# One more accumulating transfer in the first round of each attention unit, and one sum product fewer on PE

## The chip, the core and the metric

The kernel runs on one core of a Trainium2 chip. The metric is the device time of one execution in microseconds (us): the median of three runs. A profile is one further execution of the same program. The engines are named as the profile names them: PE multiplies matrices (PEld is its weight load), DVE and ACT work on vectors, POOL works on vectors and issues the software DMA queue, SP issues most of the other transfers.

## What is computed

The reference is one layer on x of shape (2, 2048, 512): a layer norm, attention with a residual, a second layer norm and a product with weights in fp8, again with a residual. The change lies in the attention alone:

```python
q = (x @ wq + bq).reshape(b, s, 16, 32)      # 16 heads of 32
k, v = ...                                   # 2 groups of 32, each shared by 8 heads
scores = einsum('bqhd,bkhd->bhqk', rope(q) * 32**-0.5, rope(k)) * 32**-0.5
attn = softmax(scores, axis=-1)
out = einsum('bhqk,bkhd->bqhd', attn, v).reshape(b, s, d)
```

The softmax is a division: the exponentials times v, over the sum of the exponentials along the keys. The change is in how that sum is formed.

## The kernel before, in words

**Units and rounds.** The queries are cut into 8 blocks of 512. A unit is 4 heads times half a block (256 queries), so there are 64 units, and the loop at L975 takes them in order. A unit goes over the 2048 keys in 16 chunks of 128, four to a round, so four rounds (r = 0 to 3, L991). I call them the first to the fourth.

**One chunk.** `probabilities` (L946) lets PE form the scores T, keys on partitions (L960), less the maximum of each query, and ACT takes the exponential into a tile `p` of 128 x 4 x 256 in float32 (L969). `columns` (L905, matmuls at L910) multiplies v by the four `p` tiles of a round and accumulates in the first half of the PSUM tile `avs`. Meanwhile the scores of the next unit are formed a second time the other way round, queries on partitions, only for their maxima (L517 on PE, L524 on DVE). These pieces (`next(scores)`) stand between the others in a fixed order.

**The sums of the exponentials.** They need the sum over all 16 chunks and over the 128 partitions.
- POOL adds chunks 0 and 1 of a round into a tile called `pair`, and chunks 2 and 3 into a tile that is kept in the list `far_sums` (`add_pair` L934, the sum at L943).
- A transfer from SBUF to SBUF, issued by POOL, adds `pair` to that kept tile (L1014, `accum_op=ALU.add`, 512 KB). So each round leaves one kept tile: `far_sums[0]` to `far_sums[3]`, named pa_2, pa_6, pa_10 and pa_14 by their chunk.
- In the third round a second such transfer adds `far_sums[0]` to `far_sums[1]` (L1016).
- Three tiles are left per unit: 1, 2 and 3. They are called `far_before` in the next unit, where PE adds them over the partitions with a matrix of ones (`sum_up` L920, the matmuls at L924) into the second half of the next unit's `avs`: tiles 1 and 2 after the columns of the first round (L1027), tile 3 after those of the second (L1029). One tile is 4 products, 8 instructions in the profile.
- `finish_heads` (L881) then copies that half (L885), takes reciprocals (L889) and multiplies (L890).

**The order.** Within the loop everything is in the order written (`manual_schedule`): each engine takes its own instructions in that order, and the semaphores hold it until what it needs is there. Small jobs of the other stages (projections, rope, the output product, statistics) are put in by `fill` (L762), at most so many pieces per place. The software queue's transfers are issued by POOL in its order, after its sums and before the job pieces of that round. SP's queue brings the next head group's queries (L355) and, at the start of a block, the next blocks of x (L141) and of its normalized form (L371).

**Buffers.** The kept tiles have four buffers, `pair` two, `p` four. A buffer is free when the last reader of its former tile is done; for a transfer that is its landing.

Of the kernel before, what the change touches and what calls it, by code (L numbers as in the profile page):

```python
# [13 lines left out]
ALU = mybir.AluOpType  # L14
# [13 lines left out]
def preln_attn_fp8_ffn_kernel(  # L28
# [37 lines left out]
    nc = tc.nc  # L66
# [42 lines left out]
    def s_bank():  # L109

        if s_next[0] == lent[0]:
            s_next[0] = (s_next[0] + 1) % S_BANKS
        tag = f"s{s_next[0]}"
        s_next[0] = (s_next[0] + 1) % S_BANKS
        return tag
# [383 lines left out]
    def split_maxima():  # L499

        if split:
            mview, mx = split.pop()
            nc.gpsimd.tensor_tensor(  # L503
                mview[:, :, :, 1], mx, mview[:, :, :, 0].bitcast(F32), ALU.subtract
            )
# [32 lines left out]
    def gather_maxima(u):  # L538

        split_maxima()  # L540
        tp = ps_s.tile([P, TB], F32, tag=s_bank(), name=f"mtp_{u}")
        for i in range(HT):
            nc.tensor.transpose(
                tp[:, i * P : (i + 1) * P], mrow[:, i * P : (i + 1) * P].bitcast(F32), ident
            )
        mT = wide.tile([P, HB], F32R, tag="mT", name=f"mT_{u}")
        nc.scalar.copy(mT, tp[:, :HB])
        maxima[u] = mT
# [213 lines left out]
    def fill(kind, pieces=1):  # L762

        for _ in range(pieces):
            ready = [job for job in queue if job.due <= step[0] and not job.waits()]
            if lent[0] is not None:
                ready = [job for job in ready if job is owner[0]]
            able = [
                (jobs, job)
                for jobs, some in ((finishing, finishing[:1]), (queue, ready), (beside, beside))  # L770
                for job in some
                if job.kind in (kind, OTHER) and job.due <= step[0]
            ]
            if able:
                do(*able[0])
# [41 lines left out]
    def stack_next(u):  # L817
        k, half = units[u]
        n, quad = quads[k]

        if half == 0:
            if k + 1 < len(quads) and k + 1 not in qst:
                while quads[k + 1] not in q_raw:
                    advance()
                stack_queries(k + 1)
            b = batch(k)
            if b + 1 < B and n == (b + 1) * NB - 1:
                if quad == 2:
                    while (b + 2) * NB - 1 not in keys_done:
                        advance()  # L830
                    fetch_keys("kS", b + 1, 0)
                    fetch_keys("dkS", b + 1, 0)
            if b > 0 and n == b * NB and quad == 0:
                fetch_keys("kS", b, 1)
                fetch_keys("dkS", b, 1)
# [84 lines left out]
    def sum_up(dst, parts, start, stop):  # L920

        for i, part in enumerate(parts):
            for j in range(4):
                nc.tensor.matmul(  # L924
                    dst[j * HD : (j + 1) * HD, :],
                    ones,
                    part[:, j, :],
                    start=start and i == 0,
                    stop=stop and i == len(parts) - 1,
                    tile_position=(0, j * HD),  # L930
                    skip_group_check=True,
                )

    def add_pair(u, kc, a, b):  # L934
        far = kc % ROUND == 2
        pa = papool.tile(
            [P, 4, HB],
            F32,
            tag="pa" if far else "pair",
            name=f"pa_{u}_{kc}",  # L940
            bufs=4 if far else 2,
        )
        nc.gpsimd.tensor_tensor(pa, a, b, ALU.add)  # L943
        return pa

    def probabilities(u, T, kc):  # L946

        k, half = units[u]
        if kc < 2:
            for j in range(4):  # L950
                nc.tensor.matmul(  # L951
                    T[:, j, :],
                    sel[:, j, :],
                    maxima[u],
                    start=(j % 2 == 0),
                    stop=True,
                    skip_group_check=True,
                )
        for j in range(0, 4, 2):
            nc.tensor.matmul(  # L960
                T[:, j : j + 2, :],
                stacked["dkS"][:, group(k), kc * P : (kc + 1) * P],
                qst[k][:, j : j + 2, half * HB : (half + 1) * HB],
                start=False,
                stop=True,
                skip_group_check=True,
            )
        p = ppool.tile([P, 4, HB], F32, tag="p", name=f"p_{u}_{kc}")
        nc.scalar.activation(p, T, AF.Exp, scale=SCALE)  # L969
        return p  # L970

    with tc.manual_schedule():
        for _ in range(LEAD):
            next(scores)
        for u, (k, half) in enumerate(units):  # L975
            n, quad = quads[k]
            if half == 0 and quad == 0:
                attn_of[n] = wide.tile(
                    [P, QUADS, TB], F32, tag="attn", name=f"attn_{n}", bufs=2
                )  # L980
            stack_next(u)
            banks = [
                ps_t.tile([P, 4, HB], F32, tag="EO"[parity], name=f"T_{u}_{parity}")
                for parity in range(2)
            ]

            far_sums = []
            whole = u == len(units) - 1
            ending_soon = u >= len(units) - 2
            pieces = 2 if ending_soon else 1  # L990
            for r in range(ROUNDS):  # L991
                chunks = list(range(r * ROUND, (r + 1) * ROUND))
                step[0] += 1
                while r == 1 and landing:
                    landing.pop()()
                if r == 2:
                    ask(u)
                last = r == ROUNDS - 1
                next(scores, None)
                probs = [probabilities(u, banks[kc % 2], kc) for kc in chunks[:2]]  # L1000
                pair = add_pair(u, chunks[0], *probs)
                next(scores, None)
                if r > 0:
                    fill(ON_PE, pieces)
                probs.append(probabilities(u, banks[0], chunks[2]))
                next(scores, None)
                probs.append(probabilities(u, banks[1], chunks[3]))
                if last and u + 1 < len(units):
                    gather_maxima(u + 1)
                if ending_soon:  # L1010
                    fill(ON_DVE)
                if not (last and whole):
                    far_sums.append(add_pair(u, chunks[2], *probs[2:]))
                    nc.gpsimd.dma_start(out=far_sums[r], in_=pair, accum_op=ALU.add)  # L1014
                if r == 2:
                    nc.gpsimd.dma_start(out=far_sums[1], in_=far_sums[0], accum_op=ALU.add)  # L1016
                fill(ON_PE, pieces)
                next(scores, None)
                split_maxima()
                fill(ON_DVE, 3 if finishing else 2)  # L1020
                if r == 0:
                    avs = ps_av.tile([P, 2, HB], F32, tag="av", name=f"avs_{u}")
                columns(u, chunks, probs, avs[:, 0, :])


                if u > 0 and r == 0:
                    sum_up(avs[:, 1, :], far_before[1:3], False, False)  # L1027
                elif u > 0 and r == 1:
                    sum_up(avs[:, 1, :], far_before[3:], False, True)  # L1029
                    finishing.append(Job(finish_heads(u - 1, both, avs[:, 1, :])))  # L1030
            both = w2.tile([P, 2, HB], F32, tag="both", name=f"both_{u}", bufs=1)
            nc.scalar.copy(both[:, 0, :], avs[:, 0, :])  # L1032
            far_before = far_sums
        sums = ps_s.tile([P, TB], F32, tag=s_bank(), name="sums_last")[:, :HB]
        sum_up(sums, [pair, *probs[2:], *far_sums[1:]], True, True)
        finishing.append(Job(finish_heads(u, both, sums)))
        fetch_y_over_keys(2, "kS", 1)
        attending[0] = False
        for jobs in (finishing, queue, beside):
            while jobs:  # L1040
                jobs[0].step()
                if jobs[0].kind is None:
                    jobs.pop(0)
# [122 lines left out]
```

## Time and profile before

| what | value |
|---|---|
| three runs | 2355.38, 2356.63, 2365.41 us; median 2356.63 |
| the profiled execution | 2365.06 us, span from first to last instruction 2363.3 us |
| mean granted PE clock | 0.969 |
| the loop over the units | about from 118 to 2260 us of the span |
| PE busy in that stretch | 2029 of 2142 us |
| DVE, ACT, POOL busy there | 1562, 1150, 1723 us |
| DMA share of the 16 engines there | 0.61 |
| L1014 and L1016 transfers | 255 and 64, 512 KB each |
| L943, one sum on POOL | 2459 ns |
| ACT waiting for a POOL sum | 19.0 us in all |

How to read it: a row of the groups gives line, engine, operation, written tile <- read tiles, shape and count; then busy time in us and mean ns of one; then the engine's idle time just before them and what ended it. A row of the timeline gives start and length in us, engine, line, operation and count, and in brackets the idle time before it with its releaser. PE's matmuls overlap, so the step from one row's start to the next row's start tells more than the length. An issue of a transfer is a short instruction on POOL or SP; "to landing" is the time from issue until the data are there.

### The profile page before, as it was taken

What the parts mean: (1) busy time and instruction counts of PE and PEld (TensorE: products, weight loads), DVE (VectorE), ACT (ScalarE), POOL (GpSimd) and SP (SyncE); (2) the same over time, 40 slices, a digit from 0 to 9 for tenths busy, and PEclk for the clock granted to TensorE, in tenths of its full rate; (3) what the DMA queues carried; (4) which work ended last, traced back from release to release, by engine and by line L of the source; (5) the groups of instructions that cost most, each with busy time, mean ns of one, the idle gap of its engine ahead of it and who ended that gap; (6) DMA issues with size and microseconds to landing.
All of it is one profiled execution on the core that took longest, in us unless ns stands there. A gap on an engine that the chain in (4) does not pass through costs nothing. (4 is left out here: it accounts for less than half of the span.)

```text
span 2363.3 us, 39392 instructions
## 1 busy us (share of the span) xinstructions
PE 2145.0 (91%) x15506; PEld 1246.7 (53%) x15506; DVE 1697.7 (72%) x2679; ACT 1231.3 (52%) x1545; POOL 1765.8 (75%) x1199
## 2 busy tenths in 40 slices
PE   5499999999999999999999999999999799899855
PEld 2255555555555555555555555555555455555422
DVE  3467777776687676867767778676876977768378
ACT  2146555655556555645445556454555445555536
POOL 3268889888777987878778878787887777878700
PEclk9689999999999999999999999999999999999977
DMA  6546656666465666657486556564565646847502
GB/s 195 163 102 136 134 117 163 137 138 136 89 167 123 152 134 143 158 116 163 96 204 139 111 118 154 121 120 96 132 146 116 143 91 140 166 85 199 108 32 111
DMA packets 116410, 312.76 MB, mean 132 GB/s; under 512 B 16896, under 2 KB 17536, under 8 KB 112384
## 3 DMA queue, kind: packets, MB, share of 16 engines
q0 software_dynamic: 50160, 175.66, 39.6%
q1 hardware_dynamic: 63648, 133.21, 19.1%
q8 instruction: 121, 1.98, 0.4%
q10 hardware_dynamic: 2416, 1.38, 0.2%
q14 instruction: 65, 0.53, 0.1%
HBM read 91.56 MB, written 42.99 MB: 57 GB/s over the span
## 5 line engine op out<-in xcount | busy, mean ns | idle before, releaser
L524 DVE TENSOR_REDUCE part<-s 128x1 f32<-128x512 f32 x2048 | 1304.8, 683 | 559.6 <-PE s L517 546.0
L943 POOL TENSOR_TENSOR pa<-p,p 128x1024 f32<-128x1024 f32 x511 | 1233.5, 2459 | 300.6 <-ACT p L969 272.7
L969 ACT ACTIVATE p<-T 128x1024 f32<-128x1024 f32 x1024 | 1001.3, 1024 | 590.6 <-PE T L960 564.1
L517 PE MATMUL s<-kS,qst 128*128 128x512 f32 x2048 | 832.4, 465 | 97.0 <-DVE part L524 31.0
L960 PE MATMUL T<-qst,dkS 128*128 128x512 f32 x2048 | 669.7, 423 | 14.4 <-ACT p L969 14.3
L517 PEld LDWEIGHTS s<-kS,qst 128*128 128x128 f32 x2048 | 369.0, 190 | 488.4 <-DVE part L524 256.9
L910 PE MATMUL avs<-p,vX 128*32 128x256 f32 x8192 | 497.7, 383 | 0.8 <-ACT p L969 0.8
L960 PEld LDWEIGHTS T<-qst,dkS 128*128 128x128 f32 x2048 | 365.5, 189 | 161.8 <-ACT p L969 59.4
L910 PEld LDWEIGHTS avs<-p,vX 128*32 128x32 f32 x8192 | 239.7, 110 | 210.4 <-issue 64.7
L1014 POOL DMA_DIRECT2D pa<-pa x255 | 224.3, 880 | 80.4 <-POOL pa L943 75.3
L889 DVE RECIPROCAL both<-both 128x128 f32<-128x128 f32 x128 | 112.4, 919 | 33.8 <-ACT both L885 33.8
L301 PE MATMUL po<-wo_sb,attn 128*128 128x512 f32 x256 | 130.5, 601 | 0.9 <-DVE x_res L574 0.9
L301 PE MATMUL pq<-xnT_q,wq_sb 128*128 128x512 f32 x224 | 113.9, 592 | 0.0
L924 PE MATMUL avs<-pa,ones 128*32 128x256 f32 x1512 | 105.6, 382 | 5.6 <-DMA pa<-pa 5.6
L1032 ACT COPY both<-avs 128x256 f32<-128x256 f32 x64 | 23.8, 373 | 138.3 <-PE avs L910 137.1
L885 ACT COPY both<-avs 128x256 f32<-128x256 f32 x63 | 23.5, 373 | 131.9 <-PE avs L924 131.9
L890 POOL TENSOR_TENSOR attn<-both 128x256 f32<-128x256 f32 x64 | 85.0, 1328 | 6.8 <-DVE both L889 6.8
L951 PEld LDWEIGHTS T<-mT,sel 128*128 128x128 f32 x512 | 80.0, 192 | 12.2 <-issue 0.4
L951 PE MATMUL T<-mT,sel 128*128 128x256 f32 x512 | 82.9, 285 | 0.0
L1016 POOL DMA_DIRECT2D pa<-pa x64 | 74.0, 1156 | 6.5 <-DMA pa<-pa 6.2
L924 PEld LDWEIGHTS avs<-pa,ones 128*32 128x32 f32 x1512 | 49.1, 111 | 39.0 <-DMA pa<-pa 6.5
L503 POOL TENSOR_TENSOR mrow<-mx,mrow 128x8 fp32r<-128x8 f32 x64 | 52.8, 824 | 11.6 <-ACT mrow L532 11.6
(126 smaller groups left out, 1118.7 us busy)
## 6 DMA issues: line engine op xcount, KB each, us to landing
pa<-pa POOLq DMA_DIRECT2D x319, 512.0 KB, 4.7
qst<-q_far SPq DMA_DIRECT2D x128, 256.0 KB, 4.7
x_kv<-in_L_attn_x_dram SPq DMA_DIRECT2D x8, 1024.0 KB, 8.8
q_far<-hi_q SPq DMA_DIRECT2D x32, 256.0 KB, 4.3
q_far<-lo_q SPq DMA_DIRECT2D x32, 256.0 KB, 3.6
x_res<-in_L_attn_x_dram SPq DMA_DIRECT2D x8, 1024.0 KB, 12.3
x_res<-in_L_attn_bo_dram POOLq DMA_DIRECT2D x8, 1024.0 KB, 12.0
out_dram<-v SPq DMA_DIRECT2D x16, 512.0 KB, 2.8
```

The source lines that it names most:

```text
L301: nc.tensor.matmul(dst, lhs(c), rhs(c), start=(c == 0), stop=(c == chunks - 1))
L517: nc.tensor.matmul(s, qst[k][:, j, at : at + P], stacked["kS"][:, group(k), kb * TB : (kb + 1) * TB], start=True, stop=True,)
L524: nc.vector.tensor_reduce(part[:, i, j, kb : kb + 1], s, AX.X, ALU.max)
L889: nc.vector.reciprocal(piece, piece)
L890: nc.gpsimd.tensor_tensor(attn_of[n][:, quad, half * HB : (half + 1) * HB], both[:, 0, :], both[:, 1, :], ALU.mult)
L910: nc.tensor.matmul(av[j * HD : (j + 1) * HD, :], vX[batch(k)][:, kc, group(k), :], p[:, j, :], start=(kc == 0), stop=(kc == NTS - 1), tile ...
L924: nc.tensor.matmul(dst[j * HD : (j + 1) * HD, :], ones, part[:, j, :], start=start and i == 0, stop=stop and i == len(parts) - 1, tile_pos ...
L943: nc.gpsimd.tensor_tensor(pa, a, b, ALU.add)
L951: nc.tensor.matmul(T[:, j, :], sel[:, j, :], maxima[u], start=(j % 2 == 0), stop=True, skip_group_check=True,)
L960: nc.tensor.matmul(T[:, j : j + 2, :], stacked["dkS"][:, group(k), kc * P : (kc + 1) * P], qst[k][:, j : j + 2, half * HB : (half + 1) * H ...
L969: nc.scalar.activation(p, T, AF.Exp, scale=SCALE)
L1014: nc.gpsimd.dma_start(out=far_sums[r], in_=pair, accum_op=ALU.add)
```

## The change

In the first round of every unit but the first, POOL issues one more accumulating transfer: the preceding unit's tile 2 (pa_10) is added to its tile 3 (pa_14), just after that round's own L1014. PE's sum product of tile 2 in the first round goes away; the product of tile 3 in the second round now reads the joined tile.

```diff
                     nc.gpsimd.dma_start(out=far_sums[r], in_=pair, accum_op=ALU.add)
+                if r == 0 and u > 0:
+
+                    nc.gpsimd.dma_start(out=far_before[3], in_=far_before[2], accum_op=ALU.add)
                 if r == 2:
                     nc.gpsimd.dma_start(out=far_sums[1], in_=far_sums[0], accum_op=ALU.add)
...
                 if u > 0 and r == 0:
-                    sum_up(avs[:, 1, :], far_before[1:3], False, False)
+                    sum_up(avs[:, 1, :], far_before[1:2], False, False)
                 elif u > 0 and r == 1:
                     sum_up(avs[:, 1, :], far_before[3:], False, True)
```

Over the 63 units that have a predecessor this is 63 more transfers of 512 KB on POOL's queue, and 504 matmul instructions fewer on PE, with as many weight loads. All other instructions stay in their order on every engine. The joined tile's product waits for the landing of the new transfer. In the changed kernel the new transfer is L1017 and the third round's second transfer moves from L1016 to L1019.

## The prediction

> **What bounds the kernel now.** I read the page first: busy shares and costliest groups, then the POOL and DMA rows that the edit touches.
>
> ```profile
> PE 2145.0 (91%) x15506; PEld 1246.7 (53%) x15506; DVE 1697.7 (72%) x2679; ACT 1231.3 (52%) x1545; POOL 1765.8 (75%) x1199
> ...
> L924 PE MATMUL avs<-pa,ones 128*32 128x256 f32 x1512 | 105.6, 382 | 5.6 <-DMA pa<-pa 5.6
> ...
> L1016 POOL DMA_DIRECT2D pa<-pa x64 | 74.0, 1156 | 6.5 <-DMA pa<-pa 6.2
> ```
>
> PE is busy 91% of the span and 9 in 10 in nearly every slice, so PE sets the pace. L924 is the line that the edit shortens: today it waits for a transfer only 5.6 us in all. Next the timeline of PE over the first two rounds of unit 27.
>
> ```profile
> 1014.36 1.93 PE L910 MATMUL avs<-p,vX 128*32 128x256 f32 x32
> 1016.11 1.05 PE L924 MATMUL avs<-pa,ones 128*32 128x256 f32 x16
> 1017.09 0.72 PE L517 MATMUL s<-kS,qst 128*128 128x512 f32 x2
> ...
> 1022.82 1.93 PE L910 MATMUL avs<-p,vX 128*32 128x256 f32 x32
> 1024.57 0.61 PE L924 MATMUL avs<-pa,ones 128*32 128x256 f32 x8
> 1025.12 0.72 PE L517 MATMUL s<-kS,qst 128*128 128x512 f32 x2
> ```
>
> Two sum products are 16 instructions and take 0.98 us until the next line's start (1017.09 - 1016.11); one takes 0.55. One product is 0.43 us.
>
> **What is removed.** 63 units x 0.43 = 27 us of PE. It shortens the run only where the others idle at that point. In each unit I took the idle time of DVE between the start of the L910 columns and its next reduce, and counted at most that: 25 us. (In three units DVE has work throughout and nothing is gained; in three it idles 0.2 or less, in the others 0.39 and more.) ACT idles over 3 us there in every unit but the last. Gain 25, bounds 15 and 27.
>
> **What is added on POOL.** 63 issues. Where one follows another issue (L1014, then L1016) POOL goes on 0.58 us later: 36 us of POOL, which is 75% busy and waits 272.7 us for ACT before its sums. Queued behind the issue are the rope or statistics of a job and the next round's first sum; ACT waits for such sums 19.0 us in all. Cost 1, bounds 0 and 5. The new issue itself waits for the last landing on the fourth sum: that had come before the place of the new issue in 62 of 63 units, in one 0.7 us after it; nothing added. The third sum's buffer is now freed by a landing instead of PE, two rounds ahead of its next use: nothing.
>
> **What is added on the path.** PE's product in the second round (the 1024.57 line) now needs the new transfer landed, and it stands in PE's order: scores, T and columns wait behind it, and DVE, ACT and POOL behind those. The time it has: from the first round's L1014 issue to that product. The time it needs: today's third round issues two transfers in the same way. The groups of L1014 and of L1016, each by its source line:
>
> ```profile
> DMA to landing us min/median/max: 4.5/4.6/14.6
> ```
>
> ```profile
> DMA to landing us min/median/max: 6.2/6.7/16.8
> ```
>
> In the 64 third rounds the second lands 2.56 us (median) after the first, and 7.13 us after the first's issue when the queues are quiet (4.55 + about 2.56). Here a rule speaks for the change. The Trainium skill, page "DMA: Bandwidth & Descriptors", section "Anatomy of one DMA — SWDGE (gpsimd) path", gives about 2.0 us fixed plus bytes over 436 GB/s: by estimate 1.2 us for each 512 KB, both landed after 4.4 us. With that the sum of waits below is 7 us and the change wins. The rows show 2.56 per transfer, more than twice, so I take the rows.
>
> Now each unit's time from L1014's issue to the product, less 0.43 because PE arrives earlier. Two patterns, from the timelines of POOL (units 25 and 27) and PE (unit 25):
>
> ```profile
> 954.34 0.86 POOL L1014 DMA_DIRECT2D pa<-pa  x1 [0.30 <-POOL pa L943]
> ...
> 1016.99 0.88 POOL L1014 DMA_DIRECT2D pa<-pa  x1 [0.30 <-POOL pa L943]
> ```
>
> ```profile
> 959.77 0.61 PE L924 MATMUL avs<-pa,ones 128*32 128x256 f32 x8
> ```
>
> Unit 27 has 7.58 us, just enough (7.58 - 0.43 = 7.15). Unit 25 has 5.43: it waits 7.13 + 0.43 - 5.43 = 2.13. Half the units have other traffic. In unit 16, SP's queue loads the next queries and two blocks, and that unit's L1014 lands after 11.6 us instead of 4.5:
>
> ```profile
> 651.77 1.86 SPq L355 DMA_DIRECT2D qst<-q_far  x4
> 653.67 0.43 SPq L141 DMA_DIRECT2D x_kv<-in_L_attn_x_dram  x1
> 654.15 0.50 SPq L371 DMA_DIRECT2D xnT_q<-xnT_far  x1
> ```
>
> The wait there is 11.56 + 2.55 + 0.43 - 7.59 = 6.95. Done for all 63 units, with landing = the larger of 7.13 and L1014's own landing + 2.55:
> - 32 quiet units (landing under 5 us): 12 with less than 7 us wait 29, the other 20 nothing to speak of: 30 us.
> - 31 units beside loads: 15 with less than 7 us wait 79, the others 45: 124 us.
>
> Together 154 us in about 42 waits. Bounds: 67 if every unit were quiet; 189 if the second transfer takes 3.2 us beside loads, as the slowest fifth of the third rounds has it.
>
> **The clock.** Such waits have a second price. Unit 58 already has one today (the timeline of PE, then the busy time by stretches: length; PE, PEld, DVE, ACT, POOL; granted clock, DMA share, GB/s):
>
> ```profile
> 2061.70 1.94 PE L924 MATMUL avs<-pa,ones 128*32 128x256 f32 x16 [5.19 <-DMA pa<-pa]
> ```
>
> ```profile
> 2061.00:2063.00 2.00, 1.30 (x15) 0.59 (x16) 0.00 (x0) 0.00 (x0) 1.21 (x1) 0.50 0.98 234
> 2063.00:2065.00 2.00, 2.00 (x11) 1.16 (x4) 0.60 (x1) 0.00 (x0) 1.70 (x2) 0.50 0.99 216
> 2065.00:2067.00 2.00, 2.00 (x9) 1.48 (x7) 1.34 (x4) 1.29 (x2) 0.33 (x1) 0.89 1.09 222
> ```
>
> After 5.19 us of waiting the clock is half until about 2065.5. From that product to the next columns is 8.33 us (2061.70 to 2070.03) against 6.71 in unit 27 (1016.11 to 1022.82): 1.6 us dearer. The Trainium skill, "TensorE: Matmul & The Clock Gate", section "Part 1: The HAM clock gate", says that an idle window of about 3.4 us halves the clock and that the window runs freely; this speaks against the change, and the row agrees for one wait. Of my 154 us, 18 waits are over 3.4 us; for a free window of that length, by estimate, 13 of them hold a whole one. 13 x 1.6 = 20 us. By the row alone, the 12 waits of 5.2 us and more: 19; with all 18 halved: 29. Bounds 15 and 29.
>
> **What comes back.** PE already idles 0.2 to 1.1 us after that product in many units; that idling can vanish in the wait: up to 12 us. Where POOL is busy without a break from before a waiting product until the next unit's L1014 (units 8, 10, 18, 26), it catches up and issues earlier: about 8. Together 20, bounds 0 and 25. Each wait ends 0.04 us after the landing, as the 2061.70 line does: 2 us. The 63 transfers bring 33 MB on top of 312.76; nobody near waits for the other loads (16.9 us on queries in all, at their start), so nothing.
>
> **Sum.** 154 + 2 + 20 + 1 - 20 - 25 = +132. The profiled execution took 2365.1 (span 2363.3), so 2497; it lay 8.4 above the median of the three runs (2356.6), so I forecast 2489 beside those runs. The rivals' times are taken down by the same 8.4.
>
> **Rivals.**
> - The transfer is hidden (faster). If a queued transfer costs the 1.2 us of the rule, both land after 4.4 us, only 7 us of waits remain, and 7 - 25 = -18 gives 2339. It decides from about 5 us after L1014's issue: there thirteen more units, with 5.4 us, begin to wait. For it: products with 7.6 us look safe. Against it: no third round's pair is landed before 7.1, and unit 16's L1014 alone takes 11.6. Chance 0.05.
> - The loads don't add up: the second transfer lands as in a quiet unit because the loads drain in between. 67 + 2 + 1 + 1 - 10 - 25 = +36: 2393. For it: L1014 itself may take the whole delay. Against it: in unit 16 the DMA share stays at 1.0 until 668. Chance 0.17.
> - The loads add up more: 189 + 2 + 24 + 1 - 8 - 25 = +183 (15 waits at half clock): 2540. For it: third rounds beside loads with 16 us to landing. Chance 0.13.
> - The main case, 2489: 0.65.
>
> **Range and chances.** 2390 to 2545 takes in the main case with its bounds, and about half of the second and third rivals. Half a per cent is about what a measurement of this kernel can tell from no change. Faster 0.05, the first rival; within it 0.03, the lower end of the second; slower 0.92.
>
> **What would show it.** Right: L924 on avs has 1008 matmuls; waits of PE at L924 for pa<-pa rise from 5.6 us to around 150 in some 40 waits, the longest 8 to 9, every second unit dearer; the clock row shows drops to half in the middle; the first round's sum block takes 0.55. Wrong: if L924's waits for the transfer stay under 30 us the hidden case holds; if they are there but the span doesn't grow, other idle time took them in; if POOL's sums or ACT's wait for POOL grow by over 20 us, the issue was the cost.

## The result, and the profile after

| | before | changed |
|---|---|---|
| median | 2359.18 us (4 runs, 2355.38 to 2365.41) | 2529.38 us (4 runs, 2528.55 to 2534.44) |
| profiled span | 2363.3 us | 2532.2 us |
| mean granted PE clock | 0.969 | 0.944 |

The change makes the kernel slower: ratio 1.0723, 95% interval 1.0694 to 1.0753. The forecast was 2489 with a range of 2390 to 2545; the direction and the place were right, the loss came out at 170 us instead of 132.

The page of the changed kernel, busy times first, then two rows of the costliest groups (busy, mean ns; idle before, releaser):

```profile
PE 2165.0 (85%) x15002; PEld 1253.4 (49%) x15002; DVE 1697.7 (67%) x2679; ACT 1232.9 (49%) x1545; POOL 1819.6 (72%) x1262
...
L924 PE MATMUL avs<-pa,ones 128*32 128x256 f32 x1008 | 86.3, 417 | 170.8 <-DMA pa<-pa 170.4
...
L1017 POOL DMA_DIRECT2D pa<-pa x63 | 73.4, 1165 | 3.2 <-DMA pa<-pa 2.8
```

PE has 504 matmuls fewer, yet its share falls from 91% to 85% because it stands still: L924's wait for the transfer went from 5.6 to 170.4 us (168.0 of it for the new transfer, 2.4 in unit 58 for an older one). The new issue on POOL hardly waits itself (3.2 us). The group of the new transfer by its source line gives its landing:

```profile
DMA to landing us min/median/max: 4.9/7.6/15.2
```

The two patterns of the prediction, from the timeline of PE, unit 25 (quiet) and unit 16 (beside loads):

```profile
1031.90 1.93 PE L910 MATMUL avs<-p,vX 128*32 128x256 f32 x32
1035.83 0.64 PE L924 MATMUL avs<-pa,ones 128*32 128x256 f32 x8 [1.99 <-DMA pa<-pa]
```

```profile
706.74 1.08 PE L924 MATMUL avs<-pa,ones 128*32 128x256 f32 x8 [7.62 <-DMA pa<-pa]
```

The idle times are 1.99 and 7.62 us; forecast were 2.13 and 6.95. The forecast counts from the time at which PE would have started the product, which adds about 0.2 us to the idle time, as shown below. In unit 16 the product itself takes 1.08 instead of 0.6 us: it runs at half clock.

**Where the time went, by round.** I took in both traces the time from each round's first L910 to the next round's (so a stretch called "third rounds" reaches up to the columns of the fourth), and summed the differences over units 0 to 62:

| stretch | after less before, us |
|---|---|
| first rounds (one product fewer) | -27.2 |
| second rounds (the wait) | +212.0 |
| third rounds | -10.2 |
| fourth rounds | -1.9 |
| before the loop, and the last unit with all after it | -5.9 and +2.1 |
| sum | +168.9 |

So the loss is in one round of four. The idle time of PE before the joined product is 168.4 us in 51 units, 163.7 of it in these rounds and 4.7 in the last unit. The other 48 us split cleanly by unit (1 to 62). Of 26 units that waited and had no more half clock than before, nearly all grew by the wait and 0.2 us. 23 units had one to three stretches of 3.4 us at half clock more than before; they grew by the wait and 1.35 us (10 units), 1.73 (4) or 2.43 (9) on the mean. The constant 0.2, some 10 us in all, is overlap that is lost: without a wait L924 starts 1.75 us after the columns (unit 27 in the prediction, 1022.82 to 1024.57), while they still run (1.93), and idle time is counted only from their end. The other 38 us go with the clock.

### The profile page after: what moved, and what is told of

Same layout as the page of the kernel before. It is cut to its first block, busy times and chain, and to the rows that moved or that the text cites. A ratio compares the mean times of both kernels' runs of the same rounds, so it can differ in the third digit from the quotient of the medians.

```text
span 2532.2 us, 38447 instructions
## 1 busy us (share of the span) xinstructions
PE 2165.0 (85%) x15002; PEld 1253.4 (49%) x15002; DVE 1697.7 (67%) x2679; ACT 1232.9 (49%) x1545; POOL 1819.6 (72%) x1262
## 5 line engine op out<-in xcount | busy, mean ns | idle before, releaser
L517 PE MATMUL s<-kS,qst 128*128 128x512 f32 x2048 | 850.2, 474 | 93.7 <-DVE part L524 31.9
L960 PE MATMUL T<-qst,dkS 128*128 128x512 f32 x2048 | 691.9, 436 | 11.2 <-ACT p L969 11.0
L517 PEld LDWEIGHTS s<-kS,qst 128*128 128x128 f32 x2048 | 380.2, 196 | 495.7 <-DVE part L524 261.3
L910 PE MATMUL avs<-p,vX 128*32 128x256 f32 x8192 | 495.7, 382 | 1.8 <-ACT p L969 1.8
L960 PEld LDWEIGHTS T<-qst,dkS 128*128 128x128 f32 x2048 | 382.4, 197 | 163.2 <-ACT p L969 56.7
L910 PEld LDWEIGHTS avs<-p,vX 128*32 128x32 f32 x8192 | 239.5, 109 | 208.9 <-issue 62.5
L1014 POOL DMA_DIRECT2D pa<-pa x255 | 224.1, 879 | 80.6 <-POOL pa L943 76.3
L924 PE MATMUL avs<-pa,ones 128*32 128x256 f32 x1008 | 86.3, 417 | 170.8 <-DMA pa<-pa 170.4
L924 PEld LDWEIGHTS avs<-pa,ones 128*32 128x32 f32 x1008 | 27.5, 113 | 209.3 <-DMA pa<-pa 198.0
L1017 POOL DMA_DIRECT2D pa<-pa x63 | 73.4, 1165 | 3.2 <-DMA pa<-pa 2.8
L1019 POOL DMA_DIRECT2D pa<-pa x64 | 75.3, 1176 | 0.2 <-issue 0.2
```

The lines of the kernel that those rows point to most:

```text
L517: nc.tensor.matmul(s, qst[k][:, j, at : at + P], stacked["kS"][:, group(k), kb * TB : (kb + 1) * TB], start=True, stop=True,)
L910: nc.tensor.matmul(av[j * HD : (j + 1) * HD, :], vX[batch(k)][:, kc, group(k), :], p[:, j, :], start=(kc == 0), stop=(kc == NTS - 1), tile ...
L924: nc.tensor.matmul(dst[j * HD : (j + 1) * HD, :], ones, part[:, j, :], start=start and i == 0, stop=stop and i == len(parts) - 1, tile_pos ...
L960: nc.tensor.matmul(T[:, j : j + 2, :], stacked["dkS"][:, group(k), kc * P : (kc + 1) * P], qst[k][:, j : j + 2, half * HB : (half + 1) * H ...
```

## The experiments

The theory: the change loses because PE stands in its order at the joined tile's product until the transfer has landed, and because these waits lower PE's clock. Rivals: the transfers' traffic and POOL's issues are the loss; a fixed price per transfer rather than its bytes; and for the part beside the waits, something other than the clock. Each run is compared with the kernel before, run beside it on the same chip.

### The transfer without anyone who waits

e1_traffic keeps the three products and adds a transfer whose result is not used:

```diff
+                if u > 0 and r == 1:
+                    nc.gpsimd.dma_start(out=far_before[2], in_=far_before[3], accum_op=ALU.add)
```

> Before, with its three products, plus one 512 KB accumulating transfer per unit that nobody waits for (it adds the preceding unit's tile 3 to its tile 2 at the start of the second round, when PE is done with tile 2; the result is not used). Wait theory: the loss of the change is PE standing at the joined tile's product, so transfer and issue alone cost 0 to 8 us: 2359 to 2367. Traffic theory (rival): 33 MB more and 63 POOL issues are the loss: above 2480.

Measured: 2379.47 against 2363.2, ratio 1.0069 (1.0043 to 1.0095). So 16 us: twice the most that I gave it, a tenth of the loss. 15.8 us of it lie in the third rounds, and 13 of these in units 8, 28, 32 and 48, which are beside loads.

e11_nobody_waits has the transfer at its right place and leaves out the joined tile's product (`sum_up(..., far_before[1:2], False, True)` and nothing in the second round); e12_no_transfer leaves out the transfer as well.

> The change, without the joined tile's product in the second round (the sums lack the chunks of tiles 2 and 3): the transfer is issued at its place and nobody on PE waits for it. Wait theory: it lies within 10 us of e12_no_transfer, near 2310 to 2320. Traffic theory: far above e12, by 50 us or more.

> As e11_nobody_waits and without the transfer: only tile 1's product is left of the three (the sums lack the chunks of tiles 2 and 3). From e2, where one product was worth 16 us: 2359 less 32 to 50, so 2310 to 2327.

Measured: e12 2323.25, ratio 0.9827 (0.9813 to 0.9842); e11 2343.4, ratio 0.9907 (0.9887 to 0.9928); before 2364.95. The transfer alone costs 20 us, again more than the 10 that I allowed, and far from the 50 and more of the traffic theory. The waits list shows where. First e12, then e11 (total us, times, longest):

```profile
PEld mtp L543 <- POOL mrow L503: 24.0, 20, 3.6
...
PE s L517 <- DMA qst<-q_far: 18.6, 3, 14.2
```

```profile
PEld mtp L543 <- POOL mrow L503: 32.5, 21, 4.9
...
PE s L517 <- DMA qst<-q_far: 26.1, 3, 14.4
```

Both are third-round waits (but for some 14 us of the second, ahead of the loop), 16 us more together: the next queries land later beside the extra 512 KB, and POOL waits with the third round's second transfer for a landing that is itself late (7.6 us in 5 units, in e12 never), which holds back L503 and with it L543 on PE. The prediction had put both at nothing. In the changed kernel itself this is not seen: its third rounds are 10 us shorter than before, L543 waits 4.7 us for L503 instead of 18.4, and no wait for the queries is left in the loop. That the long waits a round earlier give these transfers time is the likely reason; it was not tried by itself.

### What the removed product is worth

e2_dropped leaves the product of tile 2 out, without a transfer.

> The product of tile 2 is left out and no transfer takes its place, so the sums lack chunks 8 to 11. It shows what the removed product is worth. Wait theory as in the prediction: 25 us, 2334 (15 to 27 us). Rival that the removed work was hidden behind DVE and ACT: within 8 us of 2359.

Measured: 2347.09 against 2363.2, ratio 0.9932 (0.9905 to 0.9959): 16 us, in the profiles -22.6 in the first rounds and +9.2 in the third, of which 6.2 in unit 28 alone. It is near the low bound of 15 to 27. In the changed kernel the first rounds gained 27.2 (3.3 of it in unit 58, whose wait for an older transfer got shorter). So the product was on PE's path, as said.

### Half a tile

e4_half joins heads 0 and 1 alone:

```diff
-                    nc.gpsimd.dma_start(out=far_before[3], in_=far_before[2], accum_op=ALU.add)
+                    nc.gpsimd.dma_start(out=far_before[3][:, :2, :], in_=far_before[2][:, :2, :], accum_op=ALU.add)
...
                     sum_up(avs[:, 1, :], far_before[1:2], False, False)
+                    sum_up(avs[:, 1, :], far_before[2:3], False, False, (2, 3))
```

> Only heads 0 and 1 of tile 2 are joined by the transfer (256 KB); heads 2 and 3 keep their product on PE in the first round. Wait theory with a time of 2.56 us per 512 KB: the landing comes 1.28 us earlier and PE 0.2 later, so waits of 104 us in 36 units, 19 for the clock, 12 saved: 2470. Rival that a further transfer costs a fixed time whatever its size: waits stay near 168 us, 2540.

Measured: 2481.04 against 2363.2, ratio 1.0497 (1.0467 to 1.0527). From its waits list:

```profile
PE avs L924 <- DMA pa<-pa: 105.7, 35, 9.7
```

Expected were 104 us in 36 units. The landing of L1017 itself, to be set against 4.9/7.6/15.2 with the whole tile:

```profile
DMA to landing us min/median/max: 3.7/6.1/14.0
```

Unit by unit it comes 1.27 us earlier after L1014's issue (median), half of 2.56. So the time goes with the bytes, and the rival of a fixed price falls. The 11 us that the time is over the forecast are nearly the 12 us of PE that should have been saved and were not: the first rounds are 0.6 us shorter in sum. The timeline of PE shows it. A first round's sum block of e4, 12 instructions, lasts as long as one of 16 before the change:

```profile
964.84 1.05 PE L924 MATMUL avs<-pa,ones 128*32 128x256 f32 x12
```

In the trace the instructions of four heads start within 0.02 us of each other, and the next four 0.22 us after them; with two heads the next two come 0.22 us later as well. So two heads cost as much as four.

### The same join, read a round later

e3_third_round changes one figure of the change, `r == 1` to `r == 2` at the joined tile's product.

> The change as it is, but the joined tile's product stands after the columns of the third round instead of the second, some 8 us later. Wait theory: from the landings of the changed kernel only 4 units still wait, 7 us in all; 2359 - 25 + 7 = 2341, and the half-clock stretches of the loop vanish. Traffic theory: the transfers are all still there, so it stays near 2500.

Measured: 2388.49 against 2363.2, ratio 1.0106 (1.0077 to 1.0135). The loss falls from 170 to 25 us with all transfers still there, which speaks against the traffic; but 2341 was expected. The waits list names a wait that I had not counted:

```profile
ACT both L1035 <- POOL attn L890: 281.1, 62, 6.8
```

The finished heads come a round later, and their tile has one buffer, which ACT needs at the unit's end. The fourth rounds are 77 us longer. e5_third_two_buffers gives that tile `bufs=2`:

> As e3_third_round, but the tile that takes the finished heads has two buffers. In e3 no product waited for a transfer any more, but ACT waited 281 us for POOL's product of the finished heads, which came a round later and still held the only buffer. If that is the whole of what e3 lost, the fourth round's 77 us go and the time is 2310 to 2345. If the transfers themselves cost the time, it stays near 2388.

Measured: 2334.78 against 2362.2, ratio 0.9884 (0.9869 to 0.9899). It beats both kernels. But that is not the join's doing. e10_moved_only is the kernel before, without the new transfer, with the same two edits:

> Before, with all its three products and no further transfer, but tile 3's product in the third round and two buffers for the finished heads, as in e5. It shows what of e5's gain (2335) is due to the place of the product. If the join is worth its product: 2350 to 2360, at least 15 us over e5. If the place alone gains: 2335 to 2345.

Measured: 2340.16 against 2364.95, ratio 0.9899 (0.9884 to 0.9913). Nearly all of e5's gain is the place of tile 3's product: in e10 the second rounds lose 25.2 us and the third, which now hold the product, lose 2.9 as well. There PE waited for DVE anyway, as the wait of its weight load at L517 for DVE's reduces shows, first before, then e10:

```profile
PEld s L517 <- DVE part L524: 256.9, 629, 5.4
```

```profile
PEld s L517 <- DVE part L524: 215.9, 555, 2.8
```

Of these 41 us 38 are in the third rounds (72.3 to 34.4). The join itself adds 4 us by the ratios, and the intervals overlap, so no gain of its own is shown. The profiles fit that: against e10, e5's first rounds are 28.9 us shorter, and its second and third 4.1 and 18.7 longer.

### The clock by itself

e6_warm puts products by zeros on PE ahead of the joined tile's product, about 0.9 us shorter than each unit's wait, so that PE is busy while it waits for the same landing:

```diff
                 elif u > 0 and r == 1:
+                    for _ in range(IDLE.get(u, 0)):
+                        sum_up(avs[:, 1, :], [probs[3]], False, False, zeros)
                     sum_up(avs[:, 1, :], far_before[3:], False, True)
```

> The change, with products by a matrix of zeros put on PE ahead of the joined tile's product, in the 36 units that waited over 1.5 us, about 0.9 us shorter than each unit's wait (118 us of PE in all; they add nothing to the sums). The landing is what it was, so the time until the product stays; only PE is not idle. Clock theory: the 23 units at half clock lose 37 us beside their waits; most of it goes: 2495 to 2505. Rival that this loss is something else that follows a wait (engines restarting, loads): 2525 or more.

Measured: 2507.86 against 2362.2, ratio 1.0613 (1.0595 to 1.0632). More work on PE makes the kernel 22 us faster than the change (26 by the ratios; 33 between the two profiled executions, of which e6's is its fastest). The median lies just above the 2495 to 2505 that I had expected, far from the rival's 2525. The line numbers are 2 higher in this kernel; two rows of its groups:

```profile
L926 PE MATMUL avs<-p,zeros 128*32 128x256 f32 x2200 | 125.3, 379 | 0.0
...
L926 PE MATMUL avs<-pa,ones 128*32 128x256 f32 x1008 | 78.8, 384 | 54.4 <-DMA pa<-pa 53.8
```

The zeros take the place of the idle time, which falls from 170.4 to 53.8 us. The joined tile's product starts no earlier for them: from the second round's columns to it the time is the same within 1.6 us, summed over units 1 to 62. What follows the product is 37.4 us shorter, 35.5 of it in the 23 units, and the time at half clock within units 1 to 62 is 157 us less; in 22 of the 23 units it is gone. So the loss beside the waits is the clock's: about 36 of 38 us.

When does a wait cost the clock? In the changed kernel's trace all changes of the granted clock stand on one even grid with a step of 3.413 us. Below are the stretches of that grid around the waits of unit 25 (1033.83 to 1035.83) and unit 47 (1827.56 to 1829.56): length; PE, PEld, DVE, ACT, POOL; granted clock, DMA share, GB/s.

```profile
1033.51:1036.93 3.42, 1.43 (x18) 0.64 (x11) 1.24 (x5) 0.37 (x1) 3.12 (x5) 1.00 0.51 97
1036.93:1040.34 3.41, 3.41 (x9) 2.62 (x8) 2.28 (x4) 2.03 (x3) 1.23 (x3) 0.50 0.81 154
```

```profile
1825.40:1828.82 3.42, 2.16 (x33) 0.94 (x32) 2.72 (x5) 0.83 (x1) 3.42 (x2) 1.00 1.09 207
1828.82:1832.23 3.41, 2.67 (x16) 1.58 (x16) 1.45 (x3) 1.17 (x2) 1.14 (x2) 1.00 0.51 97
1832.23:1835.64 3.41, 3.16 (x29) 1.97 (x32) 3.24 (x6) 3.17 (x4) 2.17 (x1) 1.00 0.33 62
```

Both waited 2.0 us. Unit 25's wait lies in one stretch, PE is busy for 1.43 of its 3.42 us (0.42), and the next stretch has half clock. Unit 47's wait lies across a border; PE is busy 0.63 and 0.78 of the two stretches, and the clock stays. The same holds throughout. In the loops of all fourteen traces the clock fell 183 times, each time after a stretch in which PE was busy 0.54 of the time or less; it stayed full after 8045 stretches, none of them with less than 0.41. So about half a stretch of idling is enough, and for a wait shorter than a whole stretch it is a matter of luck where it lies: in the second rounds of the changed kernel all 19 waits over 3.4 us were followed by half clock, and 6 of the 16 between 1.9 and 3.0 us.

### Loads out of the way

e8_loads_later lets ACT issue the loop's loads of x and of its normalized form, in the third round where they are written; SP had run ahead with them.

> The change, with the loads of x and of its normalized form in the loop issued by ACT in its order (in the third round, where they are written) instead of by SP, which runs ahead and issues them in the first round. If these loads make the long waits, units 8, 16, 24, 32, 40, 48 and 56 fall from 6 to 10 us to about 3, 35 us of waits and 10 of clock less: 2485. If the queries' loads alone do it, no change: 2529.

Measured: 2515.51 against 2362.2, ratio 1.065 (1.0634 to 1.0666), some 14 to 17 us below the change. From its waits list:

```profile
PE avs L924 <- DMA pa<-pa: 147.1, 48, 8.1
```

23 us of waits less instead of 35. Units 16 and 24, which load two blocks, fall from 7.6 and 8.4 to 0.9 and 1.7, as expected; units 8, 40, 48 and 56 by only 0.7 to 2.9, and 32 not at all. For these I had taken the wrong loads: most of their delay is not the blocks of x. In e8's trace the queries (1 MB) are in flight beside the joining transfer in all of them, and in unit 32 also eight loads of keys (2 MB). What each of these costs was not tried.

### The join issued earlier

e7_joined_earlier issues the join in the fourth round of the unit itself:

```diff
+                if last and not whole:
+                    nc.gpsimd.dma_start(out=far_sums[2], in_=far_sums[1], accum_op=ALU.add)
```

and multiplies tile 3 in the next first round, the joined tile 2 in the second. e9_both_in_second multiplies both in the second.

> The same number of transfers and products, but the join is issued in the fourth round of the unit itself (tile 1 is added to tile 2, both long there), so the next unit's first round has the product of tile 3 alone and its second round that of the joined tile, more than a round after the issue. Wait theory: no wait is left; 27 us saved, up to 16 given back for the traffic as in e1: 2335 to 2350. Traffic theory: above 2380.

> As e7_joined_earlier, with tile 3's product moved from the first to the second round beside the joined tile's. In e7 the first round's product of tile 3 met its last landing: PE waited for transfers 20 us against 6 before, and ACT 22 us more for POOL. If that is what ate e7's gain: 27 us saved in the loop less at most 16 for the traffic, 2335 to 2350. If the joins themselves cost the 27 us, it stays at 2372.

Measured: e7 2372.04 against 2362.2, ratio 1.0049 (1.0035 to 1.0064); e9 2374.5 against 2364.95, ratio 1.0044 (1.0028 to 1.0059). Both expectations failed. The waits lists of e7, then e9:

```profile
ACT p L969 <- POOL pa L943: 37.1, 13, 12.0
...
PE avs L924 <- DMA pa<-pa: 20.4, 13, 6.5
POOL pa L1018 <- DMA pa<-pa: 19.8, 11, 8.5
```

```profile
ACT p L969 <- POOL pa L943: 42.2, 15, 11.8
...
POOL pa L1018 <- DMA pa<-pa: 16.3, 8, 8.3
```

e9 takes away PE's wait and gains nothing. POOL waits at the new issue (L1018) for the third round's transfer, up to 8 us, and ACT then waits for POOL's sums, 42.2 us against 19.0 before. By rounds e9 gains 30.7 in the first, has 25.6 more in the second for the moved product, and loses 10.1 and 5.5 in the third and fourth. Which of those is traffic and which POOL's wait, the runs don't separate.

## Why the prediction came out as it did

- **The mechanism, right.** The wait stands at L924 in the second round, waits for the transfer's landing, and holds everything behind it. e3 moves only that product and 145 of the 170 us go, although the fourth rounds grow by 77. With e5's second buffer all of the loss is gone, and what e5 gains beyond it is the better place, as e10 shows. e11 takes the product away, and the transfer is left with 20.
- **The waits: 154 us forecast, 168 measured** by PE's idle time, in 51 units instead of 42, and about 10 of lost overlap beside it, where I had 2 for the time from landing to product. Unit by unit the forecast held within 1 us in 50 of 63. It missed low where loads delayed the new transfer more than they had delayed L1014: unit 8 with 9.7 instead of 5.0, unit 28 with 8.4 instead of 4.1. The new transfer landed 2.64 us after L1014's at the median of the 30 units in which that one came within 5 us, and 2.95 in the other 33; the forecast had 2.55 for both. (Its upper bound of 189 took 3.2 us in every unit; taken only beside loads, the same working gives 173, and that rival 2524 instead of 2540.) e4 bears out a time that goes with the bytes.
- **The clock: 20 us forecast, 38 measured**: the term that was most mis-sized, and the step that failed is the count of waits, not the price. I asked for a wait that holds a whole idle window of 3.4 us and counted 13, at 1.6 us each. In the changed kernel 13 waits do hold a whole stretch of the grid without work of PE, but 23 units had more half clock than before, at 38/23 = 1.65 us each, among them units 9, 17 and 25 with waits of 1.99 us. The Trainium skill ("TensorE: Matmul & The Clock Gate", section "Part 1: The HAM clock gate") has the clock fall after an idle window of about 3.4 us, and the window run freely. The traces agree with the length and with the free run; they differ in that a window with PE busy for about half of it suffices, and the measurement decides. e6 shows that it is the clock.
- **What comes back: 20 us forecast, 12 measured** (third and fourth rounds), and not from where I had it. PE's other idling in the second rounds fell only from 16.8 to 13.4 us. Of the 12, some 8 are in the third rounds of units 28, 32, 40 and 48, beside loads.
- **The gain: 25 us forecast, 27 measured** in the first rounds with 3 of it in unit 58; e2 gives 16 for the whole run.
- **POOL's issue: 1 us, right for the changed kernel** (ACT's waits for POOL's sums fell from 19.0 to 8.9 us); "nobody near waits for the other loads" was wrong: with no wait on PE to hide it the transfer costs 16 to 20 us (e1, e11). Of the 16.9 us that PE waited for the queries before, 2.4 stood in the loop and not at the start: 1.9 in unit 28 and 0.6 in unit 32, two of the units in which the extra transfer then costs most.

Against the forecast, then: waits +14, lost overlap +8, clock +18, less coming back +8, gain -2, POOL -1, and the ends of the run -8 (5.9 ahead of the loop, and the last unit 2.6 us cheaper than its wait). That is 37 us, the difference of 168.9 in the profiles and 132. The -5.9 ahead of the loop owes nothing to the change: that stretch differs by up to 6 us among the other runs too. So misses of 11 us offset others of 48, and that is luck.

## What to carry to other kernels

A transfer that replaces work on an in-order engine is paid where its result is read, so before counting the work saved, set each use's time of need against issue plus landing, use by use and with the traffic that stands beside it. A short wait on PE can cost more than its length: here the clock fell for 3.4 us wherever PE had been idle for about half of a stretch of 3.4 us on a fixed grid, so waits of 2 us cost it or not by where they lay. And where a product has slack in its due time, moving it to a round in which the engine waits anyway can be worth more (25 us here) than removing another.

## What the runs showed of the hardware that was not expected

- The granted clock changed on a fixed grid of 3.413 us. It fell after a stretch in which PE was busy 0.54 of the time or less (183 falls in fourteen traces) and stayed after 8045 others, none under 0.41: half an idle stretch is enough, a whole one is not needed. Waits of 1.99 us cost the clock in three units, one of 2.00 us in unit 47 did not. One stretch of half clock cost 1.2 us of the round's time, three cost 2.2.
- Two of four heads of a product, side by side on the columns, took as long as four: a sum block of 12 instructions lasted 1.05 us, and so did one of 16.
- Queued accumulating transfers from SBUF to SBUF went at 2.56 us per 512 KB where they followed one another in the third rounds before; with half the size the new transfer landed 1.27 us earlier (e4, median of the units).
